# Cross-attention and a feed-forward stack on one core: masks added on TensorE, normalisations split and shared, one block's queries taken from the host's layout, look places moved

## The chip, the cores and the metric

The kernel runs on 1 core of one Trainium2 chip. The metric is the device time of one execution in microseconds (us). Three runs of the kernel before took 360.30, 356.94 and 357.82 us; the median is 357.82 us.

## The reference

The input is x, 8 batches of 256 tokens of 256 features, in f32. A cross-attention (one head, keys and values both the context, queries the normalised x) is added to x, and then a feed-forward stack with ternary weights is added to that:

```python
def attn(query, key, value, attention_mask):            # (8, 256, 256) each, mask (8, 256)
    scores = einsum('bqd,bkd->bqk', query, key) / sqrt(256)
    scores = where(causal, -inf, scores)                # k > q
    scores = where((attention_mask == 0)[:, None, :], -inf, scores)
    return einsum('bqk,bkd->bqd', softmax(scores), value)

def ffn(x):                                             # tlin(x, w, s) = einsum('bsi,oi->bso', x, w) * s
    h = silu(tlin(x, w1_w, w1_s)) * tlin(x, w2_w, w2_s) # 256 -> 1024
    h = gelu(tlin(h, h1_w, h1_s))                       # 1024 -> 1024
    h = gelu(tlin(h, h2_w, h2_s))                       # 1024 -> 1024
    return tlin(h, w3_w, w3_s)                          # 1024 -> 256

x = x + attn(layernorm(x), ctx, ctx, mask)
x = x + ffn(layernorm(x))
```

## The kernel before

**Blocks and pairs.** The 2048 tokens are four blocks (t = 0 to 3) of 512 tokens, two batches j each. Blocks 0 and 1 form pair 0, blocks 2 and 3 pair 1. Each of the two wide layers (n = 2 with h1, n = 3 with h2) is done for a pair at once as seven products of half-size matrices in place of eight; the products are called 1 to 7, and four of them use sums of quarters of the weights (S1 to S4), which VectorE (DVE) makes in `sum_up` (L660) and writes to DRAM over the SP queue (`S<-q`, L662). `stationary` (L637) fetches a product's weights over the POOL queue into one of three buffers `a`; products 1, 2 and 4 take a quarter of the weights, 3, 5, 6 and 7 one of the sums, and product 6 takes S2. f32 operands are split in two fp32r parts, high (ScalarE, ACT, L679) and low (DVE, L277), and each is multiplied.

**Units.** `pair` is a generator; what it issues between two `yield`s is a unit. In a pair, units 0 to 7 are the gated first layer of its first block (L555 to L569); 8 to 11 are product 1 of n = 2, 12 to 15 product 2, 16 to 23 the gated layer of the second block; 24 to 27 product 6, 28 to 31 product 5, 32 to 35 product 3, 36 to 39 product 7, 40 to 43 product 4. Then n = 3: 44 to 47 product 1, 48 to 51 product 6, 52 to 55 product 5, 56 to 59 product 3, 60 to 63 product 7, 64 to 67 product 2, 68 to 71 product 4; 72 to 79 are the last layer (L962). Products 7 and 4 write the same two banks `y` one after the other: after units 37 and 39 (and 41 and 43) DVE adds a bank to `nd` (`nb`), L727, and product 4 goes on in the same bank.

**Order.** Every engine's instructions are issued in the order in which the program writes them; there is no scheduler. Everything that isn't a unit (attention of the coming blocks, the sums of quarters, the "looks") is put behind a unit by a plan (`at`, `stages_at`). `stages_at(t, first, *places)` loads block t behind unit `first` and then steps its attention generator once behind each listed unit; several steps may stand behind one unit. Block 0's attention runs ahead of all units.

**Attention.** A block's `stages` takes its queries from `queries_turned` (blocks 0 and 1: normalise on DVE, transpose on TensorE as `pqt`, evacuate with 1/16 on ACT as `qt`) or `queries_loaded` (blocks 2 and 3: load x transposed from the host's array `xt`, transpose the statistics (`tma`, `hma`), write the row of means to DRAM and read it back on all partitions (`ma`, L340 and L344), subtract it on DVE (L385), and apply the reciprocal deviation to the scores). The steps of `queries_loaded` are: sums (L237); deviation on ACT; reciprocal and means' row; subtraction and `mask_bias`; then scores (`ps`, L400), masks and row maxima (L408 or L411, L420); Exp (L428); transposes and `prt` (L441 to L452); values (`pv`, L459) and x (L467); sums; normalised x and its two parts (`hyt`, `lyt`). Block 0 is worked as two groups, one for each batch, that take each step in turn; between their last transposes `keep_warm` issues multiplications by zeros.

**Loads.** `load_block` issues x (`xs`), the transposed context (`kt`), the mask (`mi`, spread to 128 partitions) and the context (`vs`) on the SP queue, in this order. `xs`, `kt` and `vs` have two buffers, `mi` has one: the mask of the next block lands where the one before is still read by `mask_bias` (L312).

**Looks.** A look (L186 to L196) reads a piece of the weights and lets ACT (Sign, L192) and DVE (L194) count entries that are not -1, 0 or 1; its result chooses at the end whether an exact second network is run. On these weights it isn't.

Of the kernel before, what the change touches and what calls it, by code (L numbers as in the profile page):

```python
# [54 lines left out]
WARM, WARM_LATER = 11, 8  # L55
# [19 lines left out]
def _network(ctx, tc, g, exact, flag):  # L75
# [30 lines left out]
    def load_block(t, behind=None):  # L106
# [4 lines left out]
        mi = new(io, [P, TB], "mi", f"mi_{t}", I32)  # L111
        span = bass.ts(t, TB)
        if behind is not None:
            for tile_ in (xs[:, 0, :1], kt[:, 0, :1], vs[:, 0, :1], mi[:, :1]):
                behind.memset(tile_, 0)
# [6 lines left out]
        for n, js in enumerate(groups(t)):  # L122
# [5 lines left out]
            if n == 0:  # L128
                nc.sync.dma_start(out=mi, in_=g.mask[:, span].to_broadcast([P, TB]))
# [32 lines left out]
    nc.gpsimd.memset(eps, EPS)  # L162
    eps256 = new(const, [P, 1], "eps256", "eps256")
# [69 lines left out]
    def sums(src, js, mv, name):  # L233

        stats = new(work, [P, NT, nc.vector.BN_STATS_DIM], "stats", f"st{name}", bufs=2)
        for i in range(NT)[tiles(js)]:
# [3 lines left out]
    def normed(src, js, mv, y, name):  # L240
# [4 lines left out]
        nc.vector.reciprocal(rstd[:, own], std[:, own])  # L245
        for i in range(NT)[own]:
            nc.vector.tensor_scalar(
# [52 lines left out]
    def table(t, js, func):  # L300

        if t == 0 and js == groups(t)[-1]:
            nc.scalar.activation(junk, eps, func)

    def near(t):

        return exact or t < 2

    def mask_bias(t, js, once, mi):
        bias = once("bias", "bias", [P, NB, SW])  # L310
        if t:
            nc.vector.tensor_scalar(  # L312
# [10 lines left out]
        for j in js:  # L323
            k0, k1 = (mi[:, j * S + k * P : j * S + (k + 1) * P] for k in range(2))
            parts = [bias[:, j, k * P : (k + 1) * P] for k in range(3)]
            nc.vector.tensor_scalar(parts[1], k0, 0.0, NEG, ALU.is_equal, ALU.mult)
            nc.gpsimd.tensor_tensor(parts[0], parts[1], causal, ALU.add)
            nc.vector.tensor_scalar(parts[2], k1, 0.0, NEG, ALU.is_equal, ALU.mult)
            nc.gpsimd.tensor_tensor(parts[2], parts[2], causal, ALU.add)
        return bias  # L330
# [17 lines left out]
    def queries_turned(t, js, once, xs, mi):  # L348
# [3 lines left out]
        sums(xs, js, mva, f"a_{t}_{js[0]}")  # L352
        yield
        y = once("y", "ya", [P, NT, D])
# [11 lines left out]
    def queries_loaded(t, js, once, xs, mi):  # L366


        mva = once("mva", "mva", [P, nc.vector.BN_AGGR_DIM, NT], bufs=2)
        sums(xs, js, mva, f"a_{t}")  # L370
        yield
# [6 lines left out]
        qt = once("qt", "qt", [P, ND, TB])  # L378
        nc.sync.dma_start(
# [716 lines left out]
```

## Time and profile before

| | us |
|---|---|
| median of 3 runs | 357.82 (356.94 to 360.30) |
| the profiled execution | 357.64 |
| its span, first to last instruction | 355.8 |
| outside the span | 1.8 |
| TensorE (PE) busy | 340.8 (96%) |
| VectorE (DVE) busy | 271.8 (76%) |
| ScalarE (ACT) busy | 218.2 (61%) |
| GpSimd (POOL) busy | 41.9 (12%) |
| first matmul of the first layer begins | 21.52 |

Times in the profile count from the span's first instruction. A row of the timeline gives start, duration, engine, line, operation and out<-in; in square brackets stands how long the engine was idle before it, and after the arrow what ended that. PEld is the weight load that runs beside the matmuls. SPq and POOLq rows are DMA issues. The profiled execution lies within 0.1% of the median, so its rows stand for a usual run.

### The profile page before, as it was taken

The numbers are of one execution on the slowest core, as the hardware profiler recorded it, in microseconds if no ns is written. First come the engines' busy times: TensorE is split into PE (matmuls) and PEld (weight loads), VectorE is DVE, ScalarE is ACT, GpSimd is POOL, SyncE is SP. The second block draws the span as 40 slices with busy tenths as digits, with TensorE's granted clock in tenths as the row PEclk, the third lists the DMA queues.
The fourth block names the chain that finished last, engine by engine and source line by source line (L and its number), as shares of the span: only waits on it lengthen the run. The fifth ranks groups of instructions, "written<-read, shape, count | busy, mean of one in ns | idle before, by whom it ended". The sixth has DMA issues, their size and how long they took to land.

```text
span 355.8 us, 4322 instructions
## 1 busy us (share of the span) xinstructions
PE 340.8 (96%) x1512; PEld 271.3 (76%) x1512; DVE 271.8 (76%) x416; ACT 218.2 (61%) x298; POOL 41.9 (12%) x73
## 2 busy tenths in 40 slices
PE   8799999999998999999999999999997999999993
PEld 3567888778877888887888878787886888888782
DVE  5868966999598947758897687589958798676771
ACT  3558733557936755757682356456995687776730
POOL 1920000320000500023000000000010000000000
PEclk9999999999999999999999999999999999999997
DMA  6799992899497944479538312950559379860032
GB/s 191 241 322 251 263 312 106 247 310 322 143 314 242 255 118 120 118 236 316 157 100 282 124 59 88 329 173 2 177 181 317 108 224 321 258 188 0 0 114 73
DMA packets 39740, 68.54 MB, mean 193 GB/s; under 512 B 2440, under 2 KB 17568, under 8 KB 39712
## 3 DMA queue, kind: packets, MB, share of 16 engines
q0 software_dynamic: 20800, 36.70, 38.9%
q1 hardware_dynamic: 18768, 31.36, 27.4%
q8 instruction: 14, 0.23, 0.3%
q14 instruction: 14, 0.11, 0.1%
q10 hardware_dynamic: 144, 0.13, 0.1%
HBM read 55.59 MB, written 8.40 MB: 180 GB/s over the span
## 4 chain that ended last, share of the span: by engine, by line
PE 79%; DVE 9%; issue 2%; ACT 1%; POOL 1%; DVEq 0%; POOLq 0%; ACTq 0%
PE px_u L696 33%; PE px_y L696 15%; PE po L962 8%; PE p L696 7%; PE pb L555 4%; PE pa L555 4%; PE ps L400 2%; PE pv L459 2%; DVE ol L277 2%; DVE T L730 2%; ACT oh L679 1%; PE pxt L265 1%; DVE hc L569 1%; DVE hd L569 1%; PE pp L441 1%
## 5 line engine op out<-in xcount | busy, mean ns | idle before, releaser
L696 PE MATMUL px_u<-ol,a 128*128 128x512 f32 x256 | 72.8, 396 | 0.9 <-DVE ol L277 0.9
L696 PE MATMUL px_u<-oh,a 128*128 128x512 f32 x256 | 73.5, 399 | 0.0
L696 PEld LDWEIGHTS px_u<-ol,a 128*128 128x128 f32 x256 | 48.1, 188 | 12.9 <-DVE ol L277 1.7
L696 PEld LDWEIGHTS px_u<-oh,a 128*128 128x128 f32 x256 | 47.8, 188 | 10.9
L696 PE MATMUL px_y<-oh,a 128*128 128x512 f32 x128 | 35.3, 398 | 3.1 <-issue 3.1
L567 ACT ACTIVATE gate<-pa,sc 128x512 f32<-128x512 f32 x32 | 21.9, 689 | 26.3 <-PE pa L555 26.1
L696 PE MATMUL px_y<-ol,a 128*128 128x512 f32 x128 | 34.9, 394 | 0.0
L637 POOL DMA_DIRECT2D a<-S x16 | 11.9, 744 | 178.9 <-PE px_u L696 55.6
L696 PEld LDWEIGHTS px_y<-oh,a 128*128 128x128 f32 x128 | 23.8, 188 | 9.4 <-issue 3.9
L696 PEld LDWEIGHTS px_y<-ol,a 128*128 128x128 f32 x128 | 24.1, 188 | 5.7
L192 ACT ACTIVATE sign<-raw 128x1024 bf16<-128x1024 f32 x16 | 16.9, 1056 | 8.1 <-DMA raw<-h1t 7.0
L555 PE MATMUL pa<-hyt,w 128*128 128x512 f32 x64 | 20.6, 403 | 0.7 <-ACT hyt L488 0.7
L555 PE MATMUL pb<-hyt,w 128*128 128x512 f32 x64 | 19.9, 391 | 0.3 <-DVE hb L569 0.3
L555 PE MATMUL pa<-lyt,w 128*128 128x512 f32 x64 | 19.9, 392 | 0.1
L555 PE MATMUL pb<-lyt,w 128*128 128x512 f32 x64 | 19.8, 390 | 0.0
L194 DVE SCALAR_TENSOR_TENSOR sign<-raw,sign 128x1024 bf16<-128x1024 f32 x16 | 19.2, 1219 | 0.2 <-ACT sign L192 0.2
L724 ACT ACTIVATE nd<-nd,sc 128x512 f32<-128x512 f32 x16 | 10.7, 716 | 13.9 <-DVE nd L727 13.9
L696 PE MATMUL p<-oh,a 128*128 128x512 f32 x64 | 17.8, 399 | 0.2 <-DVE na L727 0.2
L696 PE MATMUL p<-ol,a 128*128 128x512 f32 x64 | 17.5, 395 | 0.0
L727 DVE TENSOR_TENSOR na<-p,na 128x512 f32<-128x512 f32 x16 | 10.9, 688 | 8.5 <-PE p L696 8.5
L277 DVE TENSOR_TENSOR ol<-nT,oh 128x1024 fp32r<-128x1024 f32 x12 | 14.5, 1220 | 3.2 <-ACT oh L679 3.1
L277 DVE TENSOR_TENSOR ol<-T,oh 128x1024 fp32r<-128x1024 f32 (+1 forms) x14 | 14.6, 1069 | 2.1 <-ACT oh L679 2.0
(168 smaller groups left out, 647.2 us busy)
## 6 DMA issues: line engine op xcount, KB each, us to landing
a<-S POOLq DMA_DIRECT2D x16, 1024.0 KB, 5.5
a<-h1t POOLq DMA_DIRECT2D x6, 1024.0 KB, 8.7
a<-h2t POOLq DMA_DIRECT2D x6, 1024.0 KB, 6.7
raw<-h1t SPq DMA_DIRECT2D x8, 512.0 KB, 4.7
raw<-h2t SPq DMA_DIRECT2D x8, 512.0 KB, 4.5
vs<-ctx_n SPq DMA_DIRECT2D x4, 512.0 KB, 7.4
q<-h1t POOLq DMA_DIRECT2D x4, 512.0 KB, 21.2
q<-h2t POOLq DMA_DIRECT2D x8, 256.0 KB, 14.5
```

The costliest lines, as they stand in the source:

```text
L192: nc.scalar.activation(sign, raw, AF.Sign)
L194: nc.vector.scalar_tensor_tensor(sign, raw, 1.0, sign, ALU.mult, ALU.not_equal, accum_out=count[:, n : n + 1])
L277: nc.vector.tensor_tensor(lo, value, hi.bitcast(F32), ALU.subtract)
L400: nc.tensor.matmul(ps[:, a:e], lhsT=qt[:, c, bass.ts(2 * j + h, P)], rhs=kt[:, c, bass.ds(j * S, e - a)], start=(c == 0), stop=(c == ND - 1),)
L459: nc.tensor.matmul(pv[:, h, :], lhsT=prt[:, j, bass.ds(a + k * P, P)], rhs=vs[:, 2 * j + k, :], start=(k == 0), stop=(k == n - 1),)
L555: nc.tensor.matmul(pm, lhsT=wc[:, bass.ts(o, P)], rhs=x, start=(n == 0), stop=(n == len(steps) - 1),)
L567: nc.scalar.activation(gate, pa, AF.Silu, scale=sc[:, 0, o : o + 1])
L637: nc.gpsimd.dma_start(out=a, in_=src.rearrange("(k p) n -> p k n", p=P))
L696: nc.tensor.matmul(bank, lhsT=a[:, k, bass.ts(o, P)], rhs=x[k // 2][part][:, k % 2, :], start=start and (part, k) == steps[0], stop=stop a ...
L724: nc.scalar.activation(out, src, AF.Gelu, scale=sc[:, n, o : o + 1])
L727: nc.vector.tensor_tensor(out, one, other, ALU.add)
L962: nc.tensor.matmul(po, lhsT=w3[j * QK + k][:, bass.ts(o, P)], rhs=xs_[j][k // 2][part][:, k % 2, :], start=(j == 0 and (part, k) == STEPS[0]),
```

## The change

**Block 0.** Its mask is loaded as one row, on the ACT queue, ahead of the other loads. `mask_bias` makes one row of biases for it (0 or -1e30); the row is multiplied by a row of ones on TensorE into the scores' bank, `ident` times `causal` is added on the diagonal part, and the scores are accumulated on top. Maxima and Exp read the bank itself; the addition of L408 and the four POOL additions (L327, L329) are gone. A small POOL copy of the row's last element (into `junk`) takes their place in the queue. The sums of the fourth tile come one step later than those of the first three; the table of Exp is loaded after the first group; the first group's second normalisation is done by ACT, two activations for each tile; there are two fewer multiplications by zeros at the start (9) and one fewer later (7).

**Block 1** takes its queries by `queries_loaded`, which has one step more; it begins ahead of unit 0, and its subtraction, scores and Exp stand behind units 5, 6 and 7 (before: transposes 3, scores 4, Exp 7).

**Block 2**'s subtraction, mask, scores and Exp move from behind units 35, 45 and 46 to behind 44, 46 and 47. One sum of quarters moves from 37 to 38, and looks move, among them those behind 29, 32, 34 and 35 of pair 1 to 27, 30, 31 and 33.

```diff
-WARM, WARM_LATER = 11, 8
+WARM, WARM_LATER = 9, 7
 ...
         span = bass.ts(t, TB)
+        if t:
+            mi = new(io, [P, TB], "mi", f"mi_{t}", I32)
+        else:
+            mi = new(io, [1, TB], "mi", f"mi_{t}", I32)
+            nc.scalar.dma_start(out=mi, in_=g.mask[:, span])
 ...
-            if n == 0:
-                nc.sync.dma_start(out=mi, in_=g.mask[:, span].to_broadcast([P, TB]))
+        if t:
+            nc.sync.dma_start(out=mi, in_=g.mask[:, span].to_broadcast([P, TB]))
 ...
+    ones = new(work, [1, P], "row2", "ones_row")
+    nc.gpsimd.memset(ones, 1.0)
 ...
         nc.vector.reciprocal(rstd[:, own], std[:, own])
+        if by_scalar:
+            minus = new(work, [P, NT], "minus", f"mn{name}")
+            nc.vector.tensor_scalar(minus[:, own], mv[:, 0, own], -1.0, 0.0, ALU.mult, ALU.add)
         for i in range(NT)[own]:
+            if by_scalar:
+                nc.scalar.activation(
+                    y[:, i, :], src[:, i, :], AF.Identity, bias=minus[:, i : i + 1]
+                )
+                nc.scalar.activation(
+                    y[:, i, :], y[:, i, :], AF.Copy, scale=rstd[:, i : i + 1]
+                )
+                continue
 ...
-        if t == 0 and js == groups(t)[-1]:
+        if t == 0 and js == groups(t)[0 if func == AF.Exp else -1]:
             nc.scalar.activation(junk, eps, func)
 ...
+        own = slice(js[0] * S, (js[-1] + 1) * S)
+        row = once("bias", "maskrow", [1, TB])
+        nc.vector.tensor_scalar(row[:, own], mi[:, own], 0.0, NEG, ALU.is_equal, ALU.mult)
+        if js == groups(t)[-1]:
+            nc.gpsimd.tensor_copy(junk[:1, :], row[:, TB - 1 :])
+        return row
 ...
+        split = len(groups(t)) > 1 and js == groups(t)[-1]
+        sums(xs, js, mva, f"a_{t}_{js[0]}", slice(0, 1) if split else slice(None))
+        yield
+        if split:
+            sums(xs, js, mva, f"a_{t}_{js[0]}_1", slice(1, 2))
 ...
         sums(xs, js, mva, f"a_{t}")
+        if t == 1:
+            qt = xt_loaded()
         yield
 ...
-        queries = queries_turned if near(t) else queries_loaded
+        queries = queries_loaded if far(t) else queries_turned
 ...
+                if not t:
+                    nc.tensor.matmul(ps[:, a:e], lhsT=ones,
+                                     rhs=bias[:, bass.ds(j * S, e - a)], start=True, stop=False)
+                    nc.tensor.matmul(ps[:, e - P : e], lhsT=ident, rhs=causal, start=False, stop=False)
 ...
-            if factor is None:
+            if not t:
+                masked = ps
 ...
-        if near(t) or t == NBLK - 1:
+        if t != 2 or exact:
             y = once("y", "yf", [P, NT, D])
-            normed(xs, js, mvf, y, f"f_{t}_{js[0]}")
+            by_scalar = len(groups(t)) > 1 and js == groups(t)[0]
+            normed(xs, js, mvf, y, f"f_{t}_{js[0]}", by_scalar)
 ...
-    stages_at(1, (0, 0), (0, (0, 1, 3, 4, 7, 9, 10, 10, 10, 11, 13, 14)))
+    stages_at(1, None, (0, (0, 0, 5, 6, 7, 9, 10, 10, 10, 11, 13, 14)))
     stages_at(
-        2, (0, 8), (0, (25, 28, 30, 35, 45, 46, 49, 51, 53, 54, 55, 57, 58, 61, 62, 63))
+        2, (0, 8), (0, (25, 28, 30, 44, 46, 47, 49, 51, 53, 54, 55, 57, 58, 61, 62, 63))
     )
     stages_at(3, (0, 30), (0, (55, 56, 59, 70, 73, 74, 77)), (1, (1, 4, 8, 10, 11, 13)))
 ...
-    at(0, (32, 33, 34, 37), lambda: next(summing[4], None))
+    at(0, (32, 33, 34, 38), lambda: next(summing[4], None))
 ...
-    looks = (3, 8, 10, 11, 13, 15, 19, 26, 29, 32, 34, 35, 44, 46, 49, 51, 53, 55, 57, 58, 59)
+    looks = (3, 8, 10, 11, 13, 15, 19, 26, 27, 30, 31, 33, 44, 46, 47, 50, 51, 54, 55, 58, 59)
```

## The prediction

> **What bounds the kernel.** I read the page first, then PE's waits, then the timeline of every stretch that the change touches, engine by engine, and last the SP queue's waits.
>
> ```profile
> PE 340.8 (96%) x1512; PEld 271.3 (76%) x1512; DVE 271.8 (76%) x416; ACT 218.2 (61%) x298; POOL 41.9 (12%) x73
> PE 79%; DVE 9%; issue 2%; ACT 1%; POOL 1%; DVEq 0%; POOLq 0%; ACTq 0%
> ...
> PE px_y L696 <- issue: 3.1, 2, 1.9
> ```
>
> PE is 96% busy and holds 79% of the chain that ended last. From its first layer at 21.52 us on it stands still for little: two waits of product 4 (1.25 and 1.87, the 3.1 above) and some of 0.2 to 0.4. So any PE work removed, and any wait added, after 21.52 counts in full; ahead of it the chain through block 0's attention counts.
>
> ```profile
> 8.04 2.89 PE L400 MATMUL ps<-kt,qt 128*128 128x128 f32 x16
> 9.74 0.56 DVE L408 TENSOR_TENSOR s<-ps,bias 128x384 f32<-128x384 f32 x1 [0.36 <-POOL bias L329]
> 12.36 0.49 ACT L428 ACTIVATE s<-s,nmax 128x256 f32<-128x256 f32 x1
> 18.60 0.30 ACT L243 ACTIVATE sdf<-mvf,eps 128x2 f32<-128x2 f32 x1 [1.54 <-DVE rsf L245]
> 18.91 1.28 ACT L303 ACT_TABLE_LOAD   x1
> 20.39 1.08 ACT L488 CAST hyt<-pyt 128x512 fp32r<-128x512 f32 x2
> 21.52 0.74 PE L555 MATMUL pa<-hyt,w 128*128 128x512 f32 x2 [0.68 <-ACT hyt L488]
> ```
>
> The reader sees block 0's ladder: scores, mask addition, the last Exp, the last deviation, Silu's table, `hyt`, first layer.
>
> **1. Masks on PE: +1.3.** The 8 score products are 16 records, two for each f32 product; they follow each other by 0.112 (128 columns) and 0.216 (256). A group gains a row of 128, a diagonal of 128, a row of 256, a diagonal of 128, two records each: 6 x 0.112 + 2 x 0.216 = 1.10. The row with one partition is not in the trace; from below nothing, from above the same columns' time; I take the latter, since its columns are those of L400. Ahead of that, the split sums let the first group's normalisation go 1.1 earlier, but the second group's still ends at about 7.3 (it was 7.48), and PE takes the second group's transposes ahead of the first group's scores. So: scores 7.75 to 10.2 and 10.2 to 12.6 (1.31 + 1.10 each), ended at 12.75. Maxima (0.29, 0.41) follow at once, since L408 is gone; the second group's last Exp is 13.54 to 14.1 instead of 12.36 to 12.9. The next transposes also wait for Exp to let go of the bank: values start at 14.55, not 13.27. Removing 0.56 of DVE and the POOL wait does not pay for 1.10 on PE, twice. Bounds +0.2 (row products free) to +1.6.
>
> **2. Second normalisation of the first group on ACT: +1.9.** Its four activations (128x256, a per-partition operand; nearest row: Exp 0.49, overlapping by 0.1, dependent pairs not) take 1.8. In ACT's order the second group's deviation (18.60) comes behind them, and behind that DVE's reciprocal and the table load (18.91, the next link of the ladder). So the ladder slips 1.8 to 1.9. What it takes off DVE (0.75) was covered. Bounds +0.8 (no gaps, half the duration) to +2.3. With part 1 the first layer starts at 21.52 + 1.3 + 1.9 = 24.7. Fewer zero products cost nothing: DVE's first result is what PE then waits for. The mask's issue on ACT is over before its first deviation (4.14).
>
> **3. Block 1's queries: -1.55.** PE loses 8 transposes `pqt` (29.38 to 31.1, 1.66) and gains one `tma` (0.11). DVE swaps 1.4 of normalisation for 1.3 of subtraction and 0.4 more at the masks; ACT loses 1.1. Both have idle time here (DVE 10 of 37 us).
>
> **4. Its two new waits: +0.65 and +2.1.** The statistics (2.2 us of DVE) begin when `lyt` is done, 25.45, and end 27.6; `tma` stands in PE's queue behind unit 0, which ends at 27.0. Bounds 0 to +0.9. Then the means' row: SP has `kept` (512 KB) and now 512 KB of `xt` ahead of it. `kept` landed 11.9 us after its issue, at 34.3, behind block 1's loads; POOL's weights and these loads start 1.9 earlier now (POOL's copy writes `junk`, which ACT writes once Exp's table is in, about 8.5; the additions ended at 10.54), so 32.4; this queue moved 768 KB between 22.97 and 28.36, so `xt` takes 3.7: 36.1. In block 2 the row's read was issued 2.2 after its write and landed 5.6 later; other rows 3.4. So 39.6 or later. DVE reaches the subtraction at 37.9; 1.35 later PE may score; PE is there at 38.8. Stall 0.5 if the row is in time, 2.1 if at 39.6, 4.3 if at 41.8; I take 2.1.
>
> **5. Product 4's waits: -1.25 and -1.8.** PE's wait at 107.99 ends 0.1 after DVE's first addition on the bank that it writes next. That addition ran 2 us after its bank was full, behind subtraction and mask (101.00 to 103.26). Moved to unit 44, DVE has 2.26 less here and the addition ends ahead of PE. In pair 1 it is three counts of looks (1.14 each) in front of it, and a late Sign ahead of ACT's `oh`; two counts and two Signs leave units 32 to 35. At least nothing is gained, at most 1.25 and 1.87.
>
> **6. Block 2's scores: +0.6.** Behind unit 46 PE reaches them 5.6 after product 1 of n = 3 starts (115.50), DVE has subtracted at +6.2. Bounds 0 to 0.8.
>
> **7. What the same move does to the SP queue: +8.6.** This is the largest term.
>
> ```profile
> 94.94 0.51 SPq L124 DMA_DIRECT2D kt<-ctx_t  x1
> 102.65 0.34 SPq L129 DMA_DIRECT2D mi<-mask  x1
> 103.04 0.43 SPq L130 DMA_DIRECT2D vs<-ctx_n  x1
> 103.52 5.36 SPq L662 DMA_DIRECT2D S<-q  x4
> ...
> SPq L129 <- DVE bias L312: 7.1, 1, 7.1
> ...
> 102.20 0.42 DVE L312 TENSOR_SCALAR bias<-mi 128x512 f32<-128x512 int32 x1
> 117.97 2.49 DVE L277 TENSOR_TENSOR ol<-nT,oh 128x1024 fp32r<-128x1024 f32 x2
> ...
> 111.73 0.74 POOL L637 DMA_DIRECT2D a<-S  x1 [11.38 <-DMA S<-q]
> 125.57 1.09 PE L696 MATMUL px_u<-oh,a 128*128 128x512 f32 x4
> ```
>
> Block 3's loads stand on SP from unit 30. Its mask has one buffer and waits 7.1 us for block 2's L312, which reads the old mask. Behind it wait `vs` and the four sums of quarters, among them S2; POOL waits 11.38 for S2 (landed 111.2) and fetches product 6's weights, landed at 116.9. Product 6 begins at 125.57: 8.7 of slack. With the mask behind unit 44, DVE reads it only after `ol` (ends 120.46) and the subtraction (1.3): done at 122.1 instead of 102.6, 19.5 later. The sums themselves are made on time, but SP can't write them. Against this stand the slack 8.7, PE's 0.6 of part 6, and up to 2.0 since the weight fetch of 99.61 no longer shares the DMA engines: 19.5 - 8.7 - 0.6 - 1.6 = 8.6. Bounds: 8.2 if the whole 2.0 is won, 10.2 if nothing; below these if the mask's wait is not taken over. Product 1's weights are there, so nothing deadlocks; PE has nothing else in its queue to cover it. POOL's w3 loads are late with it; they are needed only at the last layer.
>
> **8. The clock after that wait: +2.0.** PE then stands still for over 8 us.
>
> ```profile
> 348.30:351.70 3.40, 1.46 (x7) 0.84 (x5) 1.26 (x3) 0.00 (x0) 0.00 (x0) 1.00 0.36 124
> 350.00:356.00 6.00, 0.00 (x0) 0.00 (x0) 0.67 (x2) 0.00 (x0) 0.00 (x0) 0.64 0.23 69
> ```
>
> The clock (last figure but two) averages 0.64 over 350 to 356, so it was halved at 351.7, 1.96 after the last matmul ended. At the start the products by zeros follow each other by 0.43 until 5.9 us and later ones by 0.216; transposes are at the full pace from 7.0, 5.8 after the first product. If half speed after the wait lasts as long as these two, it costs 1.0 or 2.9; I take the middle, 2.0; bounds 0 to 2.9.
>
> [...]
>
> **Sum.** 1.3 + 1.9 - 1.55 + 0.65 + 2.1 - 1.25 - 1.8 + 0.6 + 8.6 + 2.0 = 12.55. On the profiled execution's own 357.64 (span 355.8 and 1.8 around it; 0.2 under the median of the runs shown): **370.2 us**, 3.5% more.
>
> **Rivals.** (a) *SP isn't held*: `vs` and the sums pass the mask's load, so parts 7 and 8 fall: 370.2 - 10.6 = 359.6, inside the 1% that a measurement of this kernel can just tell from no change; not slower. For it: only that the load is issued 14 units ahead of the reader; against: the 7.1 us wait in the same queue now. It decides as soon as L312 ends before about 112 (8.7 and 0.6 after 102.6). (b) *Only the gains arrive*: besides (a), the start's ladder is hidden and the row comes in time: -1.55 - 1.25 - 1.8 + 0.6 + 0.5 = -3.5, 354.1. Against: at 21.52 the ladder was PE's bound. (c) *The queue is slower still*: mask, `vs` and three sums again take the 8.5 us from release to landing that they take now, the row of part 4 lands at 41.8, and the clock is halved in the emptier start too, at part 8's lower price: 370.2 + 1.6 + 2.2 + 1.0 = 375.0. For it: in the first 40 us the DMA engines are full.
>
> **Chances.** Forecast 0.72, (a) 0.13, (b) 0.05, (c) 0.10. Range: the forecast's own is 365 to 374 (parts 1 to 6 can miss by 3, 7 and 8 by 2 each); low reaches half-way to (a), 362, since part of the wait may be covered. Faster by over 1% only in (b), 0.05; within 1% in (a), 0.12; slower 0.83.
>
> **What would show it.** Each step right: `pa` starts at 24.7; Exp's last at 14; no `pqt` for block 1; L129 waits for L312 some 25 us on SP; `S<-q` of the second half of n = 3 issued during product 1 of n = 3 and not, as now, during product 7; a PE gap of 8 to 10 us ahead of product 6 of n = 3 that a landing of `a<-S` ends, and slower matmuls after it; no gap at product 4. The prediction is wrong if `S<-q` still goes out within some 10 us of its DVE sums, or if PE shows no gap over 3 us after the start.

## The result and the profile after

| | before | after |
|---|---|---|
| median of 5 runs, same chip, us | 357.8 (356.94 to 360.3) | 381.9 (378.68 to 383.19) |
| profiled execution, us | 357.64 | 378.68 |
| its span, us | 355.8 | 376.9 |
| end of the last matmul, us | 349.76 | 370.70 |

The ratio is 1.0656, with a 95% interval of 1.0592 to 1.072: slower, and by far more than the 3.5% of the forecast. The median lies above the forecast's own range (365 to 374) and above rival (c)'s 375.0. The profiled execution is the fastest of the five; this matters below. In the profile after, TensorE (PE) is busy for 10 us more, though it has little more to do, and DMA and ACT have taken shares of the chain that ended last:

```profile
PE 350.5 (93%) x1518; PEld 276.3 (73%) x1518; DVE 270.5 (72%) x412; ACT 218.9 (58%) x300; POOL 40.6 (11%) x71
...
PE 74%; DVE 12%; ACT 5%; DMA 4%; issue 4%; POOL 0%; SPq 0%; POOLq 0%; ACTq 0%; DVEq 0%
```

The waits (engine, waiting line and what it waited for: total us, times, longest) show the two largest effects. PE's first is a new one, ahead of product 6 of n = 3; SP's wait for block 2's mask is 26.3, where it was 7.1.

```profile
PE px_u L740 <- DMA a<-S: 10.3, 1, 10.3
PE ps L439 <- issue: 1.9, 1, 1.9
...
SPq L133 <- DVE bias L329: 26.3, 1, 26.3
```

The timeline of that stretch, engine by engine (start, duration, engine, line, operation; in brackets the idle time before it and what ended it):

```profile
129.15 0.42 DVE L329 TENSOR_SCALAR bias<-mi 128x512 f32<-128x512 int32 x1
...
129.59 0.34 SPq L133 DMA_DIRECT2D mi<-mask  x1
129.98 0.43 SPq L134 DMA_DIRECT2D vs<-ctx_n  x1
130.46 2.46 SPq L706 DMA_DIRECT2D S<-q  x4
...
138.75 1.48 POOL L681 DMA_DIRECT2D a<-S  x2 [29.46 <-DMA S<-q]
...
144.16 2.04 PE L740 MATMUL px_u<-oh,a 128*128 128x512 f32 x4 [10.34 <-DMA a<-S]
```

This is the chain of part 7, link by link: DVE reads block 2's mask at 129.15; only then SP may load block 3's (129.59), and behind it in the same queue go `vs` and the four sums; GpSimd (POOL) gets S2 at 138.75, the weights land at 144.02, and PE starts. The next view gives, for each window of time, its length and the busy time of each engine with the number of its instructions; the last figure but two is the granted clock, the share of its full clock that TensorE was given (0.50 is half):

```profile
144.30:149.00 4.70, 4.70 (x12) 3.63 (x13) 0.00 (x0) 0.00 (x0) 1.82 (x3) 0.50 1.46 348
149.50:154.50 5.00, 5.00 (x26) 4.10 (x26) 0.80 (x3) 1.40 (x2) 0.00 (x0) 1.00 0.72 200
```

Behind the wait the clock is at half (12 matmuls in 4.7 us; then 26 in 5.0). All halved stretches of this execution: 26.34 to 29.76, 43.41 to 46.82, 138.98 to 149.22, and after the end. Before, there was none between the opening at 6.97 and the end. All of them begin and end on one grid of 3.413 us. The clock's record begins with its first opening in an execution (5.86 here); ahead of that the zero products follow each other by 0.43, twice the 0.216 of later ones, so the clock is at half there too, though the views print 1.00.

Block 0's ladder after, to be held against the one before:

```profile
7.87 0.48 PE L430 MATMUL ps<-maskrow,ones_row 1*128 1x128 f32 x2
8.29 0.49 PE L437 MATMUL ps<-causal,ident 128*128 128x128 f32 x2
8.61 0.61 PE L439 MATMUL ps<-kt,qt 128*128 128x128 f32 x4
9.15 0.69 PE L430 MATMUL ps<-maskrow,ones_row 1*128 1x256 f32 x2
...
15.43 0.47 ACT L471 ACTIVATE s<-ps,nmax 128x256 f32<-128x256 f32 x1
...
21.88 0.51 ACT L257 ACTIVATE yf<-xs,mnf 128x256 f32<-128x256 f32 x1 [1.79 <-DVE mnf L254]
...
23.77 0.28 ACT L249 ACTIVATE sdf<-mvf,eps 128x2 f32<-128x2 f32 x1
24.07 1.28 ACT L320 ACT_TABLE_LOAD   x1
...
26.58 1.22 PE L599 MATMUL pa<-hyt,w 128*128 128x512 f32 x2 [0.96 <-ACT hyt L531]
```

The last Exp ends at 15.89 (before: 12.85) and the first layer begins at 26.58 (21.52). Following the starts of the products through the two traces, the profiled execution's delay of 20.94 at the last matmul adds up as follows:

| stretch | predicted | measured |
|---|---|---|
| to block 0's last Exp (part 1) | +1.3 | +3.04 |
| from there to the first layer (part 2) | +1.9 | +2.02 |
| to the first product of n = 2 (parts 3, 4) | +1.2 | +3.45 |
| to the last product before product 4 of n = 2 | 0 | +0.36 |
| first wait of product 4 (part 5) | -1.25 | -1.29 |
| product 1 to product 6 of n = 3 (parts 6, 7) | +9.2 | +11.02 |
| product 6 itself (part 8) | +2.0 | +2.39 |
| to product 7 of n = 2, pair 1 | 0 | +1.29 |
| second wait of product 4 (part 5) | -1.8 | -1.86 |
| to the end | 0 | +0.53 |

The two large terms are there, in their places. The other runs of the changed kernel are 2.8 to 4.5 us longer than the profiled one; experiments 1, 5 to 8, 11 and 15 are about that.

### The profile page after: what moved, and what is told of

Its sections match the earlier page's. It is cut to its first block, busy times and chain, and to the rows that moved or that the text cites. A ratio compares the mean times of both kernels' runs of the same rounds, so it can differ in the third digit from the quotient of the medians.

```text
span 376.9 us, 4343 instructions
## 1 busy us (share of the span) xinstructions
PE 350.5 (93%) x1518; PEld 276.3 (73%) x1518; DVE 270.5 (72%) x412; ACT 218.9 (58%) x300; POOL 40.6 (11%) x71
## 4 chain that ended last, share of the span: by engine, by line
PE 74%; DVE 12%; ACT 5%; DMA 4%; issue 4%; POOL 0%; SPq 0%; POOLq 0%; ACTq 0%; DVEq 0%
PE px_u L740 28%; PE px_y L740 14%; PE po L1006 8%; PE p L740 7%; PE pb L599 4%; PE pa L599 4%; PE ps L439 3%; PE pv L502 2%; DVE ol L294 2%; DVE T L774 2%; DMA S<-q 2%; ACT oh L723 2%; DMA a<-S 1%; DVE stf L243 1%; PE pxt L282 1%
## 5 line engine op out<-in xcount | busy, mean ns | idle before, releaser
L740 PE MATMUL px_u<-oh,a 128*128 128x512 f32 x256 | 75.6, 408 | 10.3 <-DMA a<-S 10.3
L740 PE MATMUL px_u<-ol,a 128*128 128x512 f32 x256 | 74.0, 401 | 0.6 <-DVE ol L294 0.6
L740 PEld LDWEIGHTS px_u<-oh,a 128*128 128x128 f32 x256 | 48.8, 193 | 22.3 <-issue 10.8
L599 PE MATMUL pb<-hyt,w 128*128 128x512 f32 x64 | 20.7, 404 | 0.2 <-DVE hb L613 0.2
L840 ACT COPY nb<-px_u 128x1024 f32<-128x1024 f32 x8 | 8.1, 1014 | 17.2 <-PE px_u L740 17.2
L740 PE MATMUL p<-oh,a 128*128 128x512 f32 x64 | 17.9, 401 | 0.1
```

The source lines that it names most:

```text
L599: nc.tensor.matmul(pm, lhsT=wc[:, bass.ts(o, P)], rhs=x, start=(n == 0), stop=(n == len(steps) - 1),)
L740: nc.tensor.matmul(bank, lhsT=a[:, k, bass.ts(o, P)], rhs=x[k // 2][part][:, k % 2, :], start=start and (part, k) == steps[0], stop=stop a ...
L840: nc.scalar.copy(mine[h], x[h])
```

## The experiments

Times are medians; the kernel before took 357.28 to 358.12 in these comparisons, in which it ran again on the same chip each time. "Base" is the changed kernel with block 3's mask loaded later (experiment 1).

**1. Block 3's mask loaded behind unit 45 (`e1_mask_later`).** The rest of the changed kernel is kept.

```diff
-        if t:
+        if t == 3 and not exact:
+            mi = None
+        elif t:
             mi = new(io, [P, TB], "mi", f"mi_{t}", I32)
 ...
-        if t:
+        if t and mi is not None:
             nc.sync.dma_start(out=mi, in_=g.mask[:, span].to_broadcast([P, TB]))
 ...
+    def mask_later():
+        xs, kt, vs, _ = loaded[3]
+        mi = new(io, [P, TB], "mi", "mi_3", I32)
+        nc.sync.dma_start(out=mi, in_=g.mask[:, bass.ts(3, TB)].to_broadcast([P, TB]))
+        loaded[3] = xs, kt, vs, mi
+    at(0, 45, mask_later)
```

> The changed kernel, with one thing taken away: block 3's mask is loaded behind unit 45, after block 2's mask has been read, and not ahead of the values and the sums of quarters in SP's queue. Theory (the queue holds the sums back, their late landing makes product 6's weights late, and PE's standstill of 10.3 us halves its clock for 5.1 more): no gap over 1 us ahead of product 6 of n = 3, no half clock there, 378.7 - 10.3 - 2.5 = 366 us; the gain at product 4 stays. Rival (the weights are late because everything ahead is 7 to 8 us later than before, or because of the moved DVE work itself): the gap stays, 376 to 379 us.

Measured: 369.54, ratio 1.0336 (1.0301 to 1.0372). The wait ahead of product 6 is gone, so the queue was its cause. The mask's load still waits for the same reader, but the sums no longer stand behind it:

```profile
111.51 8.09 SPq L708 DMA_DIRECT2D S<-q  x4
133.76 0.34 SPq L1083 DMA_DIRECT2D mi<-mask  x1
```

The total is higher than the gap alone leaves to expect, and the profiled execution (370.84) shows why: the clock was at half from 7.68 to 24.75, through all of block 0's scores, and from 34.99 to 38.40; the first layer began at 33.65. One window:

```profile
8.00:25.00 17.00, 16.18 (x47) 11.61 (x47) 2.95 (x11) 4.18 (x13) 9.11 (x18) 0.51 0.99 292
```

Rival (c) had a halved clock in the start, at a price of 1.0; 17 us of it were in no forecast. Nothing was edited ahead of unit 30, so the changed kernel's own start can do the same. The fall at 7.68 stands ahead of the first mask product, at the end of a window in which PE has little work:

```profile
4.30:7.70 3.40, 1.90 (x11) 0.88 (x9) 2.90 (x12) 1.78 (x4) 0.00 (x0) 1.00 0.89 260
8.03 0.79 PE L432 MATMUL ps<-maskrow,ones_row 1*128 1x128 f32 x2
```

**2. Block 2's steps back at 35, 45, 46 (`e2_block2_back`)**, the rest as changed.

> The changed kernel with block 2's subtraction, mask, scores and Exp put back behind units 35, 45 and 46. Theory (queue): the gap and its half clock go, product 4's wait of about 1.3 comes back: 378.7 - 12.8 + 1.3 = 367 us. Rival (lateness of what stands ahead): the gap stays, 378 us.

Measured: 370.57, ratio 1.0322 (1.0238 to 1.0406), runs from 365.25 to 370.71. No wait ahead of product 6; the first wait of product 4 is back (1.08); half clock from 8.06 to 25.13 in the profiled execution (370.71). Two different cures of the queue end at the same time.

**3. Block 2's move alone, on the kernel before (`e3_move_alone`).**

```diff
-        2, (0, 8), (0, (25, 28, 30, 35, 45, 46, 49, 51, 53, 54, 55, 57, 58, 61, 62, 63))
+        2, (0, 8), (0, (25, 28, 30, 44, 46, 47, 49, 51, 53, 54, 55, 57, 58, 61, 62, 63))
```

> The kernel before with only block 2's four steps moved behind units 44, 46 and 47. Theory (queue): the same gap of about 10 us ahead of product 6 and 1 to 3 us of half clock after it, product 4's first wait of 1.25 gone: 357.6 + 10.3 + 2.5 - 1.2 = 369 us. Rival: without the late start the weights are in time, 356 to 357 us.

Measured: 369.32, ratio 1.0331 (1.0295 to 1.0366). Twelve microseconds from one line of places. Its waits:

```profile
PE px_u L696 <- DMA a<-S: 10.4, 1, 10.4
...
SPq L129 <- DVE bias L312: 24.8, 1, 24.8
```

The same hold and the same gap as in the full change, with the start of the kernel before: part 7 needs nothing of the rest. In its trace the sums went out from 120.82 on, S2 was there at 129.1, and the weights landed at 134.47; the clock was at half from 126.78 to 140.43.

**4. The same move with block 3's mask later (`e4_move_mask_later`).**

> The kernel before with block 2's four steps moved as in the change, and block 3's mask loaded behind unit 45. Theory (queue): nothing is held, only product 4's first wait goes: 357.6 - 1.2 + 0.1 = 356.5 us. If 357.6 or more, the gain at product 4 is given back later.

Measured: 357.57, ratio 1.0007 (0.9985 to 1.003). The hold costs nothing once the mask is out of the queue's way, and the move gains nothing: the first wait of product 4 is gone (its start goes from 0.50 late to 0.91 early), but product 6 of n = 3 starts only 0.48 early, the product after it 0.07. Against the 0.50 by which this execution was late from block 0 on (there PE waited 1.1 for `kt` to land), 1.4 were won, and 0.8 of them are given back within two products: 0.5 where block 2's scores now stand, which is part 6, and 0.4 in product 6. The 0.6 that is left is less than the totals can show.

**5. The start kept busier, on the base (`f1_start_filled`).**

```diff
-WARM, WARM_LATER = 9, 7
+WARM, WARM_LATER = 11, 8
 ...
             nc.scalar.activation(qt[:, c, cols], pt, AF.Copy, scale=1.0 / 16.0)
+        if t == 0 and js == (0,):
+            keep_warm(4)
```

> The changed kernel with block 3's mask loaded behind unit 45 (369.5 us, first layer at 33.65 with half clock from 7.7 to 24.8), and TensorE kept busier at the start: 11 and 8 zero products as before, and 4 more between block 0's two groups of transposes, in the wait of 0.98. Theory (the emptier start lets the clock fall): no half clock between 8 and 25, first layer at 26 to 27.5, total 362 to 363.5. Rival (the score stretch itself, with its one-row products, counts as idle, whatever is ahead of it): half clock still there, first layer at 33 or later, total 369 to 371.

Measured: 364.96 (364.33 to 365.13), ratio 1.021 (1.017 to 1.0249). No half clock before the end; first layer at 26.52. The same window as in experiment 1:

```profile
8.00:25.00 17.00, 13.79 (x70) 9.43 (x70) 7.40 (x27) 7.48 (x20) 9.10 (x18) 1.00 1.00 299
```

So the halved clock in the start was worth 4.6 us of median (369.54 to 364.96), and a few multiplications by zeros in a wait prevented it here. The total is 1.5 us above the upper end of what was expected: the first layer's 5.0 is still there, and 1.9 more between it and n = 2 (experiment 10).

**6. Block 0's masks as before, on the base (`f2_masks_back`)**: mask to all partitions on SP, added by DVE, combined on POOL; still 9 and 7 zero products.

> The same base with only block 0's masks as before (added by VectorE, combined on GpSimd, mask loaded to all partitions by SyncE), still 9 and 7 zero products. Theory (the mask products on TensorE, through their sparse use of it, keep the clock down): clock stays full through the scores, last Exp of block 0 near 13, first layer near 23.5 (21.5 and 1.9 for the normalisation on ACT), total 359 to 361. Rival (9 zero products are too few by themselves): half clock from about 8 still there, first layer above 29, total 365 to 369.

Measured: 365.45, ratio 1.0216 (1.0176 to 1.0257). The 17 us of half clock are gone, last Exp at 13.82, first layer at 24.53; but 23.69 to 30.52 and 44.17 to 47.58 are at half, and the total is 4.5 us above the theory's upper end. The theory holds for the scores, and its total doesn't.

**7. The second normalisation back on DVE, on the base (`f3_norm_back`).**

```diff
-            by_scalar = len(groups(t)) > 1 and js == groups(t)[0]
+            by_scalar = False
```

> The same base with only the first group's second normalisation back on VectorE. Prediction's part 2 (ACT's four activations lengthen the ladder): first layer 1.9 earlier relative to the last Exp, total 367.5 to 368. Rival (at half clock the activations hide behind TensorE): no change, 369 to 370.

Measured: 369.25, ratio 1.0325 (1.0283 to 1.0366). The halved start (8.16 to 25.23) is there again. The first layer comes 2.04 earlier than in experiment 1, as part 2 has it, but n = 2 starts 1.06 later, with a half-clock stretch from 49.12 on; the total hardly moves. Experiment 13 repeats this with the start filled.

**8. Mask products with operands of 128 partitions, on the base (`f4_full_rows`)**; the sum is the same.

```diff
-    ones = new(work, [1, P], "row2", "ones_row")
+    ones = new(work, [P, P], "row2", "ones_row")
     nc.gpsimd.memset(ones, 1.0)
+    row0 = new(work, [P, TB], "bias", "maskrow")
+    nc.gpsimd.memset(row0, 0.0)
 ...
-        row = once("bias", "maskrow", [1, TB])
-        nc.vector.tensor_scalar(row[:, own], mi[:, own], 0.0, NEG, ALU.is_equal, ALU.mult)
+        row = row0
+        nc.vector.tensor_scalar(row[:1, own], mi[:, own], 0.0, NEG, ALU.is_equal, ALU.mult)
 ...
```

> The same base, but the mask product uses operands of 128 partitions (the mask in partition 0, zeros in the others, all ones as stationary) in place of one partition; the sum is the same. Theory (a one-partition stationary makes its weight load visible, 0.21 and 0.31 per record): records 0.11 and 0.22 as the scores' own, block 0's scores 0.6 us shorter a group at full clock; if the one-row products also kept the clock down, half clock gone and total 360 to 362. Rival (the switch of weights costs the same whatever the rows, and the clock is down for want of zero products): same durations, total 369 to 370.

Measured: 365.17 (364.55 to 365.6), ratio 1.0218 (1.0178 to 1.0258).

```profile
7.69 0.39 PE L434 MATMUL ps<-maskrow,ones_row 128*128 128x128 f32 x2
7.92 0.39 PE L441 MATMUL ps<-causal,ident 128*128 128x128 f32 x2
8.14 0.61 PE L443 MATMUL ps<-kt,qt 128*128 128x128 f32 x4
8.59 0.60 PE L434 MATMUL ps<-maskrow,ones_row 128*128 128x256 f32 x2
...
10.11 0.38 PE L434 MATMUL ps<-maskrow,ones_row 128*128 128x128 f32 x2
```

Count from the first mask product of one group to that of the next: 7.69 to 10.11, 2.42 us; in the changed kernel 7.87 to 11.06, 3.19. With 1.31 for the scores themselves, a group's masks cost 1.11 with full operands and 1.88 with one-partition operands, though they compute the same and move the same columns. Single records show where it goes: with one partition, the next weight load begins when the matmul ahead of it is nearly over (the load at 9.148 behind the matmul that began at 8.945; the row products start 0.21 apart), with 128 partitions it begins under the matmul (at 8.476 under the one from 8.474; 0.11 apart). The load itself takes nearly the same (0.18 us with one partition, 0.19 with 128); what differs is when it starts. The last Exp ends at 14.26 (+1.41), the first layer begins at 24.96 (+3.43), and the 17 us of half clock are not in the profiled execution, nor, by their totals (364.55 to 365.6) and mean clocks (0.986 to 0.993), in the other three; two windows of 3.41 are at half in it (from 24.96 and from 42.03). The window ahead of its scores, at nearly the same place as in experiment 1, holds little more work, and no fall follows:

```profile
4.30:7.70 3.40, 2.10 (x12) 0.98 (x11) 2.84 (x12) 1.78 (x4) 0.00 (x0) 1.00 0.81 248
```

**9. The looks and the last sum alone, on the kernel before (`g1_looks_alone`).**

```diff
-    at(0, (32, 33, 34, 37), lambda: next(summing[4], None))
+    at(0, (32, 33, 34, 38), lambda: next(summing[4], None))
-    looks = (3, 8, 10, 11, 13, 15, 19, 26, 29, 32, 34, 35, 44, 46, 49, 51, 53, 55, 57, 58, 59)
+    looks = (3, 8, 10, 11, 13, 15, 19, 26, 27, 30, 31, 33, 44, 46, 47, 50, 51, 54, 55, 58, 59)
```

> The kernel before with only the looks of pair 1 and the last sum of quarters at their new places. Prediction's part 5: the second wait of product 4 (1.87 at 274.84) goes, DVE's addition being in time; that product starts 1.3 to 1.8 earlier against the first of pair 1, and the total falls to 355.5 to 356.2. Rival (the gain is given back later in pair 1, as the first wait's gain was by product 6): the wait is gone, the total stays within 0.5 of the kernel before.

Measured over 12 runs: 356.44, ratio 0.9956 (0.9935 to 0.9977). The 1.87 ahead of product 4 of pair 1 is gone; only the 1.3 of pair 0 is left among PE's waits on `px_y`:

```profile
PE px_y L696 <- issue: 1.3, 1, 1.3
```

A new wait of 0.56 for ACT stands ahead of product 7, and the net is -1.3 in this trace, all of which reaches the end. The 1.87 could cost more than its length: in the traces of experiments 3 and 15, where that wait stands, a window of 3.41 at half begins about 1 us behind it (287.20 and 276.62), in the kernel before none does. With the wait gone, no mean clock of the 12 executions is under 0.994; of the kernel before 4 of 17 have 0.990 or 0.991 and take 358.88 to 359.88. That they are executions with such a window is argued from this.

**10. Block 1's queries alone, on the kernel before (`g2_queries1_alone`)**: `queries_loaded` at the changed kernel's places.

```diff
-        queries = queries_turned if near(t) else queries_loaded
+        queries = queries_loaded if t and not exact else queries_turned
 ...
-    stages_at(1, (0, 0), (0, (0, 1, 3, 4, 7, 9, 10, 10, 10, 11, 13, 14)))
+    stages_at(1, None, (0, (0, 0, 5, 6, 7, 9, 10, 10, 10, 11, 13, 14)))
```

> The kernel before with only block 1's queries from the host's layout, at their new places. Prediction's parts 3 and 4: -1.55 on TensorE, +0.65 at the means' transpose, +2.1 at the scores, so the first product of n = 2 starts 1.2 later and the total is near 358.6. Theory from the trace of the changed kernel and the run with the filled start (there the stretch from first layer to that product is 1.9 longer than before): total 359 to 360, more if a clock period is halved behind the wait (1.7). Rival (only the prediction's 1.55 arrives): 356.

Measured: 366.48, ratio 1.0257 (1.0224 to 1.0291). All three expectations fell. Its waits, and its timeline of the same place:

```profile
DVE qt L392 <- DMA ma<-ma: 6.4, 1, 6.4
PE ps L407 <- DVE qt L392: 6.4, 1, 6.4
```

```profile
27.32 0.35 SPq L340 DMA_DIRECT2D ma<-hma  x1
36.70 0.36 SPq L344 DMA_DIRECT2D ma<-ma  x1
...
42.94 4.61 PE L407 MATMUL ps<-kt,qt 128*128 128x128 f32 x16 [6.37 <-DVE qt L392]
```

The row of means is written at 27.32, and its reading is issued 9.4 us later, when that write has landed; `xt` landed at 36.96. The row is there at 42.13. In the changed kernel the write is issued at 31.41, 4.1 later, and the row is there at 42.53, nearly the same time. So it is not the start's ladder that dates this row here. The DMA engines are full (their busy share is 1.07 and more from 11 to 25 us in the profile after, and 1.23 from 38 to 43 here; in the kernel before, whose first 40 us rival (c) called full, 1.16 and 1.21 in the last two tens of them, 0.60 and 0.85 in the first two), and that is the likely cause; no run takes load off them. The date holds only for starts like these: in eight traces with the first layer at 21.6 to 27.0 DVE begins the subtraction at 41.2 to 43.2, but in experiments 1, 2 and 7, with the first layer at 31.6 to 33.7, at 47.5 to 48.1. PE was ready for the scores at 36.6 here and, having been held up by the ladder, at 41.5 in the changed kernel. The wait is 6.4 in the one and 1.9 in the other: the lateness of the start paid for most of block 1's price. Behind the 6.4 the clock is at half (39.54 to 46.37), and the scores take 4.6 us.

**11 and 12. The gap ahead of product 6, left and filled.** `h1_held_filled` is the changed kernel, with the mask in the sums' way, and the start filled as in 5. `h2_gap_filled` adds useless products:

```diff
+    def filled():
+        fill = ps_mm.tile([P, TB], F32, tag="mm", name="fill")
+        for _ in range(42):
+            nc.tensor.matmul(fill, lhsT=w1[0][:, :P], rhs=w1[1][:, :TB], start=True, stop=True)
+    at(0, 47, filled)
```

> The changed kernel as it is (block 3's mask in front of the sums on SyncE's queue) with the filled start (11 and 8 zero products and 4 more between the groups' transposes). Theory: the filled start takes off what it took off without the queue's hold, 4.5 from the median, and the queue's hold is worth its gap and the halved clock behind it: 365.0 (run with the mask later) + 8.5 to 10.3 + 2.5 = 376 to 377.8. Rival (hold and start overlap, because a later start of everything eats slack): below 374.

> The same with 42 useless products of 512 columns (9.1 us) behind unit 47, in the gap ahead of product 6. Their result goes nowhere. Theory (part 8: the gap lowers the clock, and this costs 2.5): no half clock behind the gap, total 2 to 2.5 less than the kernel with the held queue and the filled start. Rival (product 6 is slow there for another cause, its operands or weights): no change, or more where the useless products outlast the wait.

Measured: 378.9, ratio 1.0588 (1.0546 to 1.063), and 376.46, ratio 1.051 (1.0468 to 1.0552). Windows behind the gap, first of the kernel with it, then of the kernel with it filled:

```profile
144.50:149.30 4.80, 4.80 (x12) 3.73 (x13) 0.00 (x0) 0.00 (x0) 1.81 (x3) 0.50 1.42 343
```

```profile
145.20:150.00 4.80, 4.80 (x24) 3.98 (x25) 0.16 (x1) 0.82 (x1) 1.81 (x3) 1.00 1.48 356
```

Twice the matmuls in the same time, and 2.4 us of median: part 8 is a halved clock, and is priced. From start to start product 6 takes 12.82 with the gap and 10.61 with it filled. The total of 378.9 is above the 376 to 377.8 expected: the gap is 10.47, and in this profile the clock was also at half from 26.44 and from 43.51, 3.41 each, though the start was filled as in experiment 5. The filled start keeps the clock through the scores; whether it falls later differs between executions. Against the changed kernel itself, which differs from `h1_held_filled` by nothing but these zero products, the median falls by 3.0, from 381.9 to 378.9 (four of its five executions lie above all four of these, though the intervals of the two ratios just overlap). That is near the 3.2 by which the changed kernel's median lies above its profiled execution. The two profiled executions have the same time (378.68) and the same three halved stretches to 0.1 us.

**13. The start filled and the second normalisation on DVE, on the base (`k2_filled_norm_back`).**

> The kernel with the filled start and the mask loaded later (365.0), and the first group's second normalisation back on VectorE. Theory (block 1's means' row lands at 42.1 to 42.5 whatever the start does, so it sets the time): first layer at 24.5 instead of 26.5, the wait for the row grows from 2.1 to about 4, total within 0.5 of 365.0. Rival (the ladder to the first layer counts in full, as the prediction had it): 363.0.

Measured: 363.44 (361.56 to 364.91), ratio 1.0141 (1.0095 to 1.0186). The four times go with their mean clock: 364.34 and 364.91 at 0.985, 362.53 at 0.990, 361.56 at 0.998; experiment 5 had 364.33 to 365.13 at 0.994 to 0.996. In the profiled one (364.34) the row landed at 41.23, the wait for it was 2.87, and the clock was at half from 41.39 to 48.22. The median lies nearer to the rival's 363.0 than to the theory's 365.0. So the theory's "within 0.5" is wrong where the clock holds, and what the shorter ladder gains can be lost again to the clock behind the longer wait. With four runs this is a reading, not a measurement of each half.

**14. Start filled, block 1's queries as before, on the base (`k4_filled_queries_back`).**

> The kernel with the filled start and the mask loaded later (365.0), and block 1's queries as before, turned on TensorE at their old places. Theory of the row: the wait of 2.1 and the means' transpose go, TensorE has 1.55 more work, the first layer's 5.0 remains: first product of n = 2 about 5 later than before instead of 6.9, total 362.5 to 363.5. Prediction's parts 3 and 4 (queries of block 1 cost 1.2 net): 363.8. Rival (the row's wait was hidden, the removed work counts): 366.5.

Measured: 362.98, ratio 1.0137 (1.0102 to 1.0172): 2.0 less than experiment 5, as the theory of the row has it, and 2.8 less when each is held against the kernel before of its own comparison. With a late start, block 1's queries cost 2 to 3 us; with the start of before, 8.7 (experiment 10).

**15. Fewer zero products alone, on the kernel before (`k1_fewer_zeros`).**

> The kernel before with only 9 and 7 zero products in place of 11 and 8. Theory (the clock falls in the start for the fewer zeros together with the one-row mask products): alone they do nothing, no half clock after the first 7 us, 357 to 358.5. Rival (the fewer zeros alone let the clock fall): half clock within the first 25 us, 361 to 366.

Measured: 358.97 (357.31 to 360.44), ratio 1.0022 (0.9997 to 1.0048). In the profiled execution the clock opened at 10.38, one window later than in the kernel before (6.97 and 3.41), whose grid it shares, so that most of block 0's scores ran at half:

```profile
7.96 4.05 PE L400 MATMUL ps<-kt,qt 128*128 128x128 f32 x16
```

They took 2.89 before. The first layer begins at 22.58, 1.06 later than before, so in this execution the fewer zeros alone did cost; the median can't tell it from nothing. Once open, the clock held until 276.62 (experiment 9). The 17 us aren't there, and no total of the ten is 4 us above the kernel before: the fewer zeros alone don't make them.

**16. Block 2's move, block 3's mask later, looks and sum moved, on the kernel before (`k3_move_later_looks`).**

> The kernel before with block 2's move, block 3's mask loaded behind it, and the looks and the last sum moved. Theory (the first wait's gain is given back by product 6, the second's arrives): 355.9 to 356.4, as with the looks alone. Rival (the first gain arrives too): 355.0 to 355.3.

Measured: 355.39 (354.8 to 356.3), ratio 0.9928 (0.9903 to 0.9953). Its interval lies below 1; against experiment 9 alone the intervals overlap, so the totals leave open whether the move adds anything. Its trace shows what experiment 4's does: 0.62 late ahead of product 4 of pair 0, 0.81 early at it, 0.04 late behind product 6 of n = 3. So 0.6 of the first gain stays, on top of a start that was 0.6 late; product 4 of pair 1 then starts 1.45 early.

## Why the prediction was wrong

The sign, the place and the mechanism of the largest term were right, and rivals (a) and (b) are out; (c)'s halved start was the nearest to what came, but with the wrong size. The sum was 11.7 too low: 8.5 in the profiled execution and 3.2 between it and the median.

- **Part 1 failed by its own choice of a row** (+1.3, at most +1.6; measured +3.04). For the product of one partition it took "the same columns' time", and called that the upper bound. Experiment 8 shows that this is right for full operands (1.11 a group against the 1.10 worked out, +1.41 at the last Exp, +3.43 at the first layer against 3.2) and that one partition costs 0.77 a group more, since the weight loads no longer run under the matmuls. The trace of before has no such switch, so the upper end should have added a weight load (0.18) to each one.
- **Part 2 was right** (+1.9; +2.02).
- **"Fewer zero products cost nothing" was the step that failed most.** It looked at PE's waits alone; the zero products are there for the clock. Put back, with four more, into the changed kernel, they take 3.0 off its median (experiment 11), and 4.4 to 4.6 without the queue's hold (experiment 5). What they end in experiment 1 is seen: 17 us at half clock, through all of the scores. In the profiled execution of the changed kernel this didn't happen. For its other four runs there is only the mean clock: 0.951 to 0.962, against 0.974. At 0.957 that is about 13 us more of half clock (0.017 x 2 x 380), as 17.07 in place of 3.41 would make; that their start is that of experiment 1 is argued from this and not seen in a trace, and one run of experiment 2 (370.49 at 0.996) doesn't fit such a reckoning. What brings the clock down stays open. Three different edits end the 17 us: more zeros (5), no mask products (6), or full-row mask products (8); fewer zeros alone don't make them (15). But the window at whose end the clock falls holds 1.9 us of products and is over within 0.1 us of the first mask product's start or ahead of it (7.68 and 8.03, 8.06 and 8.04, 8.16 and 8.08 in experiments 1, 2 and 7), so by these records the one-row products can at most keep it down, and why a window with 2.1 us ahead of full rows is not followed by a fall isn't shown. The prediction had a halved clock in the emptier start only in rival (c), at 1.0, and not in its sum.
- **Parts 3 and 4** (+1.2; measured +3.45). The wait for the row was 1.9, near the 2.1 taken, but for the wrong reason: row and PE were both later than worked out, the row at 42.5 instead of 39.6, PE at 41.5 instead of 38.8. PE began the scores 0.8 behind the row, when half of the subtraction was done, and not 1.35. (By the rate it gives, `xt` takes 3.6 and not 3.7.) Within the range of these starts, the row's date hardly follows the start (experiment 10). 1.5 of the rest is clock: with the start filled and no halving (experiment 5), the same stretch is +1.9.
- **Parts 5 and 6**: the first wait gave its 1.29, and 1.4 in experiments 4 and 16. Of that, 0.5 goes back where block 2's scores stand, near part 6's 0.6, and 0.4 in product 6 of n = 3, which no part had; 0.6 is left, near the forecast's 0.65 for the two, in part by luck, since the 0.4 makes up for a gain that was larger than forecast. The addition ran 3.6 us after its bank was full (103.02 to 106.67), not 2; nothing hangs on it. The second wait gave 1.86 at its place and 1.3 net (experiment 9).
- **Parts 6 and 7** (+9.2; +11.02; the gap itself 8.6 against 10.3). The release was met: DVE read the mask at 129.15, that is 122.1 plus the 7.6 by which everything ran late there. What failed is the credit of 1.6 for a faster weight fetch: from the mask's issue to landed weights it took 14.4 (129.59 to 144.02), and before 14.25 (102.65 to 116.9). The fetch of 99.61 is away, but POOL now issues the fetches of two sums together (138.75) and six loads of `w3` right behind; that these took its place on the DMA engines is argued. Without the credit the sum gives 10.2, which was the upper bound; measured 10.3 to 10.5 in three kernels. The 0.7 between the gap and the stretch is block 2's scores (part 6).
- **Part 8** (+2.0; 2.39 in the trace, 2.2 to 2.4 by filling the gap) was right.
- Not foreseen at all, and not explained further: 1.29 from product 6 of n = 3 to product 7 of pair 1, of which some 0.7 is the looks' own new wait (experiment 9), and 0.5 up to the end.

## What to carry to other kernels

A load on an in-order queue is priced by what stands behind it: one mask whose buffer is freed late cost 12 of the 24 us here (381.9 to 369.54, experiment 1), and issuing it 15 units later cost nothing (357.57 against 357.43, experiment 4). Multiplications by zeros and dense neighbours made a difference here to the clock of the work behind them (17 us at half in experiment 1, none of that with more zeros in 5 or full rows in 8): before such work is taken away or made sparser, look in the trace for the steps of the clock around it, which lay on a grid of 3.413 us here, and at what PE does between them, and take several runs, since the clock differs between executions of one program (a mean of 0.951 to 0.974 in the five of the changed kernel). And prices measured one by one do not add when they wait for the same date: a late start hid most of block 1's price.

## What the runs showed of the hardware that was not expected

- In the changed kernel a matmul whose operands have one partition, among full ones, costs 0.21 us a record at 128 columns where a full one costs 0.11, and the full one behind it is held back too (0.21 from its start at 8.285 to the next); filling the other 127 partitions with zeros removes this (1.88 to 1.11 us a group, experiment 8).
- Half clock lasted while PE was hardly idle: in experiment 1 PE is 16.18 of 17 us busy by its records from 8 to 25, at 0.51, and without a break from 7.7 to 17.9, while in the kernel before it opened at 6.97, behind a window with 3.02 of 3.41 (3.56 to 6.97). Busy time in the profile thus doesn't by itself tell when the clock opens. In experiment 1 it opened at 24.75, behind 2.7 us of the value products of 256 columns, which started at 22.06; what opens it isn't shown.
- All falls and openings of one execution lie on a grid of 3.413 us (experiment 1: 4.27, 7.68, 24.75, 34.99, 38.40), and its phase is not the same in every trace: the opening at 6.97 in the kernel before lies 0.71 ahead of a step of experiment 1's grid.
- The wait of 1.9 ahead of block 1's scores is followed by a halved window in one execution (43.41 to 46.82 in the profile after) and one of 2.1 in another is not (experiment 5). The same holds for the wait ahead of product 4 of pair 1: 1.87 without one in the kernel before, 1.80 and 1.86 with one in experiments 3 and 15.
